# A depthwise tap moved from VectorE to a ScalarE product and an accumulating DMA, with a matrix streamed to make room

**Chip, cores, metric.** One core of one Trainium2 chip. The metric is the time of one execution in microseconds of device time, the median of several runs.

## The reference, cut to what matters

Input x is 32 images of 96 channels on 56 x 56 points. Three layers follow each other; the change touches the first, and one matrix of the second.

```python
# layer 0: expand 96 -> 576, depthwise 3x3, project 576 -> 96, residual
h = relu(bn(einsum('oc,bchw->bohw', w1, x)))
h = dwconv3x3(h, wdw)                  # nine taps per channel
h = relu(bn(h))
x = x + bn(einsum('oc,bchw->bohw', w2, h))
# layer 1a: layernorm, linear+relu, FFT over the 3136 tokens, a weighting with relu, inverse FFT, linear
# layer 1b: layernorm, a quantised two-layer MLP
```

## The kernel before

The 576 hidden channels are four groups of 128 on VectorE ("units") and a last group of 64 that TensorE does with diagonal matrices. A unit is one half image (28 rows, so 1568 points per channel) of one group: 8 units per image, 256 in all. Everything is written as generators that advance in common "ticks"; a unit takes four ticks, an image 32. Beside the units run the jobs of other images: `front` (projection, normalisation, transposes, start of the transform), `mid` (mixer), `back` (MLP).

```python
class Unit:
    def tap(self, n):                       # TAPS[0] is the centre (0, 0)
        dr, dc = TAPS[n]
        if n == 0:
            self.acc = ... w1.tile([128, R, S], F32, name="acc", bufs=7)
        ...                                 # rows ra:rb, columns ca:cb that the tap covers
        if n == 0:
            nc.scalar.activation(dst, src, AF.Identity, scale=w, bias=bd[...])
        else:
            nc.vector.scalar_tensor_tensor(dst, src, w, dst, ALU.mult, ALU.add)
    def finish(self):
        nc.scalar.activation(self.acc, self.acc, AF.Relu)

for u, after in zip(units, units[1:] + [None]):
    for q in range(4):                      # one tick each
        if q < 2 and after: after.expand(q)         # TensorE products, relu on ScalarE
        if q == 0 and last: last.finish()
        if q == 3 and after: after.tap(0)
        u.tap(2 * q + 1)
        u.tap(2 * q + 2)
        ...                                 # loads of the next image's halves, cut
        yield
    last = u

# front, cut: the projection reads the finished accumulators (and ends with an eviction on ScalarE),
# the norm is a chain of small VectorE and ScalarE steps, then TensorE transposes its result
#   pw <- w2T, acc | xt <- pw | bn_stats, va, sda, ra | xn <- xt, ra | ps <- ident, xn

jobs.append((T * i + 16 * (u // 2 + 1) + 1 + 4 * (u % 2), front(i, u)))
```

Two words used below: an *eviction* is the instruction (here mostly on ScalarE) that copies a TensorE result out of the tile TensorE wrote it to (`hs<-ps`, 128x812, took 936 ns in the kernel before); a DMA's *landing* is the time at which its data has arrived.

The text that is written gives an order to each engine only in part: the builder's scheduler moves instructions on an engine against each other where data allows. The traces are read here as each engine keeping the order of the list that comes out.

## Time and profile before

| | before |
|---|---|
| time | 5533.3 us, median of 3 runs (5532.4 to 5535.3) |
| TensorE busy | 4965 us, 90% |
| VectorE busy | 5018 us, 91% |
| ScalarE busy | 3801 us, 69% |
| mean granted TensorE clock | 0.955 of full speed |

The granted TensorE clock, in tenths, over 40 equal slices of the span:

```profile
PEclk9899999999999999999999999999999999999986
```

### The profile page before, as it was taken

To read this page: it belongs to the slowest core of one execution; us is meant where nothing else is said; L and a number is where in the kernel's file an instruction comes from. 1 tells how busy PE (TensorE), PEld (TensorE's weight loads), DVE (VectorE), ACT (ScalarE), POOL (GpSimd) and SP (SyncE) were. 2 spreads that over 40 slices of the span, in tenths; PEclk is the share of its full clock that TensorE was granted. 3 is DMA by queue.
4 is the path that set the end of the run, shared out by engine and by line. 5 is a ranking of instruction groups with operands and counts; after the bars stand their busy time and mean duration, and the time that the engine had idled before them with its cause. 6 is when DMAs were issued, how large, how long until landed. Compare 5 with 4: busy or idle time off the path is not lost.

```text
span 5533.0 us, 83297 instructions
## 1 busy us (share of the span) xinstructions
PE 4965.2 (90%) x32464; PEld 3804.1 (69%) x32464; DVE 5018.1 (91%) x8008; ACT 3800.6 (69%) x5574; POOL 75.6 (1%) x138
## 2 busy tenths in 40 slices
PE   5888999999999999999999999999999999999987
PEld 3566766766766766766766766766766767767765
DVE  7889999999999999999999999999999999999953
ACT  2456776776776776776777776776776777776765
POOL 0000000000000000000000000000000000000000
PEclk9899999999999999999999999999999999999986
DMA  2112332322232232232322332322332322332232
GB/s 51 48 50 64 86 87 74 86 85 77 81 88 79 82 87 79 82 87 78 87 84 76 85 88 74 88 83 77 86 87 76 88 81 77 88 84 78 78 106 66
DMA packets 320146, 440.94 MB, mean 80 GB/s; under 512 B 128244, under 2 KB 229176, under 8 KB 319640
## 3 DMA queue, kind: packets, MB, share of 16 engines
q1 hardware_dynamic: 319752, 435.62, 28.2%
q8 instruction: 255, 4.18, 0.3%
q14 instruction: 139, 1.14, 0.1%
HBM read 242.85 MB, written 192.68 MB: 79 GB/s over the span
## 4 chain that ended last, share of the span: by engine, by line
PE 77%; ACT 12%; DVE 7%; issue 2%; DMA 2%; SPq 0%; ACTq 0%
PE pd L459 13%; PE pw L511 13%; PE ps L351 12%; DVE acc L379 5%; PE ps L546 5%; PE ps L607 4%; PE ps L558 4%; PE ps L674 3%; PE ps L715 3%; ACT u L724 3%; PE ps L663 3%; PE pw L519 3%; PE ps L767 2%; PE ps L749 2%; PE ps L536 2%
## 5 line engine op out<-in xcount | busy, mean ns | idle before, releaser
L379 DVE SCALAR_TENSOR_TENSOR acc<-hs,wdw,acc 128x1540 f32<-128x1540 f32 (+3 forms) x2048 | 3674.1, 1799 | 55.3 <-ACT acc L377 48.2
L511 PE MATMUL pw<-w2T,acc 128*112 128x96 f32 x7168 | 912.9, 266 | 219.0 <-ACT acc L382 172.7
L511 PEld LDWEIGHTS pw<-w2T,acc 128*112 128x112 f32 x7168 | 824.2, 179 | 311.2 <-ACT acc L382 190.5
L351 PE MATMUL ps<-xs,w1T 96*128 96x406 f32 x2048 | 845.7, 533 | 21.5 <-ACT hs L358 17.5
L459 PE MATMUL pd<-hl,diag 128*128 128x385 f32 (+1 forms) x2304 | 825.4, 493 | 4.8 <-ACT al L468 1.8
L358 ACT ACTIVATE hs<-ps,b 128x812 f32<-128x812 f32 x512 | 479.2, 936 | 226.6 <-PE ps L351 176.7
L459 PEld LDWEIGHTS pd<-hl,diag 128*128 128x128 f32 x2304 | 420.6, 190 | 266.3 <-issue 39.3
L351 PEld LDWEIGHTS ps<-xs,w1T 96*128 96x128 f32 x2048 | 378.0, 201 | 196.7 <-issue 141.9
L377 ACT ACTIVATE acc<-hs,bd,wdw 128x1568 f32<-128x1568 f32 x256 | 434.9, 1699 | 4.3
L382 ACT ACTIVATE acc<-acc 128x1568 f32<-128x1568 f32 x256 | 385.3, 1505 | 42.7 <-DVE acc L379 42.6
L761 ACT ACTIVATE h<-h 128x784 fp8e5<-128x784 f16 x384 | 327.2, 855 | 79.0 <-DVE h L760 55.0
L724 ACT ACTIVATE u<-tt,mf,rf 112x96 fp8e5<-112x96 f32 x896 | 334.7, 454 | 55.8 <-DVE mf L494 55.6
L757 ACT ACTIVATE h<-ps 128x784 f16<-128x784 f32 x384 | 314.0, 820 | 60.2 <-PE ps L749 60.0
L546 PE MATMUL ps<-watt,xnT 97*112 97x192 f32 x1792 | 349.5, 334 | 1.8 <-ACT xnT L537 1.8
L558 PE MATMUL ps<-z,wa 112*112 112x384 f32 (+1 forms) x1024 | 344.0, 455 | 3.0 <-ACT z L550 2.9
L546 PEld LDWEIGHTS ps<-watt,xnT 97*112 97x112 f32 x1792 | 307.1, 183 | 50.2 <-issue 22.0
L607 PEld LDWEIGHTS ps<-wb,yb 112*128 112x128 f32 (+1 forms) x3584 | 308.5, 167 | 47.2 <-ACT h L757 18.4
L607 PE MATMUL ps<-wb,yb 112*128 112x112 f32 (+1 forms) x3584 | 329.5, 272 | 1.1 <-ACT y L771 0.8
L511 PE MATMUL pw<-w2T,al 128*112 128x96 f32 x1792 | 325.4, 264 | 0.0
L519 PE MATMUL pw<-idb,xs 97*112 97x96 f32 x1792 | 323.9, 263 | 0.0
L717 DVE TENSOR_TENSOR tt<-tt,ps 112x672 f32<-112x672 f32 x128 | 108.9, 851 | 214.1 <-PE ps L715 214.1
L537 ACT ACTIVATE xnT<-ps 96x784 f32<-96x784 f32 x128 | 104.6, 817 | 278.4 <-PE ps L536 278.2
(164 smaller groups left out, 7071.8 us busy)
## 6 DMA issues: line engine op xcount, KB each, us to landing
ydr<-ya SPq DMA_DIRECT2D x512, 147.0 KB
yb<-ydr SPq DMA_DIRECT2D x128, 588.0 KB
wd<-in_wd_dram SPq DMA_DIRECT2D x128, 349.1 KB
xs<-in_x_dram SPq DMA_DIRECT2D x64, 609.0 KB
tdr<-xt SPq DMA_DIRECT2D x128, 294.0 KB
tt<-tdr SPq DMA_DIRECT2D x128, 294.0 KB
gdr<-gc SPq DMA_DIRECT2D x256, 147.0 KB
gd<-gdr SPq DMA_DIRECT2D x128, 294.0 KB
```

What stands on the lines that cost most here:

```text
L351: nc.tensor.matmul(ps[:, j, 0:QW], lhsT=w1T[:, 128 * self.k : 128 * (self.k + 1)], rhs=xs[self.img, self.s][0:C, at : at + QW], start=True ...
L358: nc.scalar.activation(flat[:, 2 * h * QW : 2 * (h + 1) * QW].rearrange("p (j w) -> p j w", j=2), ps[:, :, 0:QW], AF.Relu, bias=b1[:, self ...
L377: nc.scalar.activation(dst, src, AF.Identity, scale=w, bias=bd[:, self.k : self.k + 1])
L379: nc.vector.scalar_tensor_tensor(dst, src, w, dst, ALU.mult, ALU.add)
L382: nc.scalar.activation(self.acc, self.acc, AF.Relu)
L459: nc.tensor.matmul(pv[:, :, ca:cb], lhsT=diag[:, n, :], rhs=hl[:, q : q + 7, ca + dc : cb + dc], start=(n == 0), stop=(n == 8),)
L511: nc.tensor.matmul(ps[:, q - a, 0:C], lhsT=src.rearrange("p r c -> p (r c)")[:, at : at + SK], rhs=w2T[:, k + (s if k == NK else 0), :], s ...
L519: nc.tensor.matmul(ps[:, q - a, 0:C], lhsT=xs[img, s][:, at : at + SK], rhs=idb, start=False, stop=True)
L546: nc.tensor.matmul(pv[0:SK, q - a, 0:HA], lhsT=xnT[:, q * SK : (q + 1) * SK], rhs=watt, start=True, stop=True)
L558: nc.tensor.matmul(ps[0:SK, j, 0 : (e - q) * HA], lhsT=wa, rhs=z[:, q:e, :], start=True, stop=True)
L607: nc.tensor.matmul(o, lhsT=lhsT, rhs=wb[:, g0 + G * s + q, :], start=True, stop=True)
L724: nc.scalar.activation(u8[:, q, :], t[:, q, :], AF.Identity, scale=r[:, q : q + 1], bias=m[:, q : q + 1], saturate=False,)
```

## The change

Intent: take one of eight taps off VectorE. The centre tap becomes a plain ScalarE product into a tile of its own, and an accumulating DMA adds that tile to the accumulator when the other taps are done. The vertical tap that covers all rows, until now VectorE's, becomes the ScalarE instruction that begins the accumulator. Since the accumulator is ready only when the DMA has landed, relu and front jobs move two ticks later, which needs an eighth accumulator; one of the input loads moves a tick later too. The room for the new tiles comes from streaming the transform matrix wb per mixer job and from single buffers for wd and gc.

```diff
+        def begin(self):
+            self.acc = ... w1.tile([128, R, S], F32, name="acc", bufs=8)
+            dr = 1 - 2 * self.s
+            nc.scalar.activation(self.acc, self.hs[:, o : o + R, :], AF.Identity, scale=self.weight(dr, 0), bias=...)
+        def centre(self):
+            self.p = w1.tile([128, R, S], F32, name="centre")
+            nc.scalar.activation(self.p, self.hs[:, o : o + R, :], AF.Copy, scale=self.weight(0, 0))
+        def taps(self, q):
+            ...                              # two of the seven remaining taps per tick
+            if q == 3:
+                nc.gpsimd.dma_start(out=self.acc..., in_=self.p..., accum_op=ALU.add)
...
+                if q == 1:
+                    u.centre()
-                if q == 0 and last:
+                if q == 2 and last:
                     last.finish()
...
+        yield
+        yield
         last.finish()
...
-    wb = cst([SK, NP, SK], "wb")            # whole matrix, loaded once
+        wb = w1.tile([SK, 2 * G, SK], F32, name="wb")    # in mid: one half, loaded per job
-            gc = w2.tile(...)
+            gc = w1.tile(...)
-        wd = w2.tile(...)
+        wd = w1.tile(...)
-            jobs.append((T * i + 16 * (u // 2 + 1) + 1 + 4 * (u % 2), front(i, u)))
+            jobs.append((T * i + 16 * (u // 2 + 1) + 3 + 4 * (u % 2), front(i, u)))
```

More of the change, by code (lines that the diff above doesn't have):

```diff
@@ L192, in tile_kernel @@
     ws = load([SK, SK], "ws", d["ws"])
-    wb = cst([SK, NP, SK], "wb")
-    nc.sync.dma_start(out=wb.rearrange("p k m -> p (k m)"), in_=d["wb"])
     b1 = cst([128, NK + 1], "b1")
@@ L363, in expand, with weight @@
             )
-        def tap(self, n):
-            dr, dc = TAPS[n]
-            o = R * self.s - base[self.s]
-            if n == 0:
-                self.acc = acc[self.img, self.s, self.k] = w1.tile([128, R, S], F32, name="acc", bufs=7)
-            at = 3 * (dr + 1) + dc + 1
-            w = wdw[:, self.k, at : at + 1]
-            ra, rb = max(0, -(o + dr)), min(R, XR - o - dr)
-            ca, cb = max(0, -dc), S - max(0, dc)
-            src = self.hs[:, ra + o + dr : rb + o + dr, ca + dc : cb + dc]
-            dst = self.acc[:, ra:rb, ca:cb]
-            if n == 0:
-                nc.scalar.activation(dst, src, AF.Identity, scale=w, bias=bd[:, self.k : self.k + 1])
-            else:
-                nc.vector.scalar_tensor_tensor(dst, src, w, dst, ALU.mult, ALU.add)
+        def weight(self, dr, dc):
+            at = 3 * (dr + 1) + dc + 1
+            return wdw[:, self.k, at : at + 1]
@@ new lines, in begin @@
+        def begin(self):
+            self.acc = acc[self.img, self.s, self.k] = w1.tile([128, R, S], F32, name="acc", bufs=8)
+            dr = 1 - 2 * self.s
+            o = R * self.s - base[self.s] + dr
+            nc.scalar.activation(
+                self.acc,
+                self.hs[:, o : o + R, :],
+                AF.Identity,
+                scale=self.weight(dr, 0),
+                bias=bd[:, self.k : self.k + 1],
+            )
+        def centre(self):
+            self.p = w1.tile([128, R, S], F32, name="centre")
+            o = R * self.s - base[self.s]
+            nc.scalar.activation(self.p, self.hs[:, o : o + R, :], AF.Copy, scale=self.weight(0, 0))
@@ new lines, in taps @@
+        def taps(self, q):
+            rest = [t for t in TAPS[1:] if t != (1 - 2 * self.s, 0)]
+            o = R * self.s - base[self.s]
+            for dr, dc in rest[2 * q : 2 * q + 2]:
+                ra, rb = max(0, -(o + dr)), min(R, XR - o - dr)
+                ca, cb = max(0, -dc), S - max(0, dc)
+                src = self.hs[:, ra + o + dr : rb + o + dr, ca + dc : cb + dc]
+                dst = self.acc[:, ra:rb, ca:cb]
+                nc.vector.scalar_tensor_tensor(dst, src, self.weight(dr, dc), dst, ALU.mult, ALU.add)
+            if q == 3:
+                nc.gpsimd.dma_start(
+                    out=self.acc.rearrange("p r c -> p (r c)"),
+                    in_=self.p.rearrange("p r c -> p (r c)"),
+                    accum_op=ALU.add,
+                )
@@ L389, in conv_ticks @@
         units[0].expand(1)
-        units[0].tap(0)
+        units[0].begin()
         last = None
@@ L395, in conv_ticks @@
                     after.expand(q)
-                if q == 0 and last:
+                if q == 1:
+                    u.centre()
+                if q == 2 and last:
                     last.finish()
                 if q == 3 and after:
-                    after.tap(0)
-                u.tap(2 * q + 1)
-                u.tap(2 * q + 2)
+                    after.begin()
+                u.taps(q)
                 if q == 2 and u.s == 0 and u.k == NK - 1 and u.img + 1 < nimg:
                     load_half(u.img + 1, 0)
-                if q == 2 and u.s == 1 and u.k == NK - 2 and u.img + 1 < nimg:
+                if q == 3 and u.s == 1 and u.k == NK - 2 and u.img + 1 < nimg:
                     load_half(u.img + 1, 1)
@@ L586, in mid @@
         g0 = 2 * G * half
+        wb = w1.tile([SK, 2 * G, SK], F32, name="wb")
+        nc.sync.dma_start(
+            out=wb.rearrange("p k m -> p (k m)"), in_=d["wb"][:, g0 * SK : (g0 + 2 * G) * SK]
+        )
         yb = []
@@ L606, in spread @@
                         o, lhsT = pv[:, q, 0:SK], yb[s][:, q, 0:128]
-                    nc.tensor.matmul(o, lhsT=lhsT, rhs=wb[:, g0 + G * s + q, :], start=True, stop=True)
+                    nc.tensor.matmul(o, lhsT=lhsT, rhs=wb[:, G * s + q, :], start=True, stop=True)
             return pv[:, 0:G, 0:SK]
@@ L693, in mid @@
             nc.tensor.matmul(ps[0:SK, 1, 0:n], lhsT=wc, rhs=p[:, n:], start=True, stop=True)
-            gc = w2.tile([SK, G * C], F32, name="gc")
+            gc = w1.tile([SK, G * C], F32, name="gc")
             nc.scalar.activation(gc.rearrange("p (j w) -> p j w", j=2), ps[0:SK, :, 0:n], AF.Copy)
@@ L704, in back @@
     def back(img, u):
-        wd = w2.tile([KD, G * SK], F32, name="wd")
+        wd = w1.tile([KD, G * SK], F32, name="wd")
         nc.sync.dma_start(out=wd, in_=d["wd"][:, G * SK * u : G * SK * (u + 1)])
```

## The prediction

The forecast came to 166.7 us per image, 5340 us in all. Its sum has 14 us of stalls per image, reckoned with L, the DMA's time from issue to landing, at 7.5 us (between 6 and 9).

> **What bounds the kernel now.** I read the page's first part (busy shares), then a table of stretches, one image long each, then the groups by shape, then the waits, and last the chain of work inside a stretch of 60 us. The program runs 32 images of equal work as one software pipeline; start-up and drain aside an image takes about 173 us (5533 / 32).[...]
>
> ```profile
> PE 4965.2 (90%) x32464; PEld 3804.1 (69%) x32464; DVE 5018.1 (91%) x8008; ACT 3800.6 (69%) x5574; POOL 75.6 (1%) x138
> ...
> q1 hardware_dynamic: 319752, 435.62, 28.2%
> ```
>
> ```profile
> core 0: us, PE busy (x) PEld busy (x) DVE busy (x) ACT busy (x) POOL busy (x), PEclk, DMA share, GB/s
> ...
> 2173.00:2346.00 173.00, 159.88 (x1074) 123.47 (x1073) 163.79 (x268) 122.72 (x180) 2.19 (x4) 0.98 0.30 85
> 2346.00:2519.00 173.00, 159.88 (x1062) 123.13 (x1060) 162.64 (x263) 122.81 (x180) 2.20 (x4) 0.97 0.29 82
> ```
>
> Two engines are full: of 173 us VectorE is busy about 162.5 and TensorE 160. ScalarE has 50 us of room, GpSimd does nothing, the DMA engines are 29% busy. The groups by shape say what VectorE does:
>
> ```profile
> L379 DVE SCALAR_TENSOR_TENSOR acc<-hs,wdw,acc 128x1540 f32<-128x1540 f32 x1024 | 1852.2, 1812 | 20.3 <-ACT acc L377 16.9
> ...
> L379 DVE SCALAR_TENSOR_TENSOR acc<-hs,wdw,acc 128x1568 f32<-128x1568 f32 x256 | 472.5, 1846 | 1.2
> ...
> L377 ACT ACTIVATE acc<-hs,bd,wdw 128x1568 f32<-128x1568 f32 x256 | 434.9, 1699 | 4.3
> ...
> L382 ACT ACTIVATE acc<-acc 128x1568 f32<-128x1568 f32 x256 | 385.3, 1505 | 42.7 <-DVE acc L379 42.6
> ```
>
> Eight of nine taps of each of the 256 depthwise units (8 per image) are VectorE work. The waits show that TensorE's gaps come mostly from lateness there: the projection waits for a finished accumulator, a transpose for a normalised tile.
>
> ```profile
> PEld pw L511 <- ACT acc L382: 190.5, 41, 9.0
> ...
> PE pw L511 <- ACT acc L382: 172.7, 37, 8.8
> ...
> PE ps L536 <- DVE xn L531: 104.4, 35, 6.4
> ```
>
> But TensorE's busy time is not all throughput. In the chain of one stretch its pieces touch, and give the real pace:
>
> ```profile
> 2010.61 1.95 PE pd L459 x6
> 2012.56 0.97 PE pw L511 x10
> ...
> 2015.58 1.38 PE ps L351 x4
> 2016.96 1.36 PE ps L674 x14
> ```
>
> Six L459 products take 1.95 us, 0.325 us each, where the group's mean for one is 493 ns (the modelled ends overlap). Summing the groups at such paces (L459 72 x 0.325, L351 64 x 0.345, the projection 336 x 0.098, the other products about 68 us) I get some 147 us per image that TensorE needs. So VectorE is the bound by need, 162.5, and TensorE follows with 147 to 160.
>
> [...]
>
> **The change part by part.** (1) VectorE loses the full-size tap: 8 x 1.846 = 14.8 us per image, so need 162.5 - 14.8 = 147.7. The vertical tap that covers all rows becomes the first ScalarE product, at the same 1568 elements, so no change there. (2) ScalarE gains a Copy with a scale over 1568 elements, between the relu's 1.505 and the begin's 1.699: 8 x 1.6 = 12.8 us, so 123 + 13 = 136 us. That is beside other work by sum, but in its queue. (3) A DMA of 128 x 1568 x 4 = 803 KB per unit. Queue 1 moved 435.62 MB in 28.2% of the 16 engines' 5533 us: 279 GB/s while busy. A copy of 803 KB at that rate is 2.9 us[...]. (4) The product buffer is single, so the next unit's centre product waits for this DMA to land; the relu stands right behind it in ScalarE's order. That wait is the real cost. In the built order of the changed kernel I followed it for the eight units of an image: from a unit's last tap, add up the VectorE work that stands ahead of the first VectorE instruction that needs ScalarE work after the next centre, and take off the ScalarE work between, at the durations above. That leaves room for L of 5.0, 6.1, 2.8, 5.5, 11.9, 6.7, 7.1 and 5.5 us. What L exceeds stalls VectorE: at 6 us 5 us per image, at 7.5 us 14, at 9 us 24. (5) The wb matrix streamed: 64 x 702 KB = 45 MB more, asked for three ticks (16 us) before use, on a queue with room: nothing. wd with one buffer: nothing, since the gd tile loaded beside it is single already and is released by the same products. gc with one buffer: ScalarE may wait for the first store of a pair, one tick (5.4 us) earlier; up to 1 us, twice per image. The front jobs' two ticks later keep the distance to the later relu; eight accumulators pay for it.
>
> **Sum.** Before: 162.5 of need plus 10.5 of VectorE's idle = 173. After: 147.7 of need, 14 of stalls on the DMA, and of the 10.5 idle perhaps 5, because ScalarE's and TensorE's lateness hides behind the same stalls (this is a choice, not a measurement). 166.7 us per image, 6.3 less; over about 31 images in steady state 195 us: **5340 us**, 3.5% faster.
>
> **The rivals.** (A) The DMA is quick, 6 us or less: stalls fall to 5 us, need is 147.7 beside TensorE's 147, and TensorE becomes the bound near 160: about 5130 to 5200. For it: [...]DMA engines idle two thirds of the time. (B) The DMA takes 9 us or more: 147.7 + 24 + 4 = 176 us, so 5600 to 5650, and at 10 us (31 of stalls) over 5800; the wait at the centre product takes the place of the tap removed. For it: [...]the present traffic comes on bursts of 73% share. Against it: the single buffer would hardly have been kept had the wait been that long. (C) TensorE is the bound already, as the page's chain (77% TensorE) suggests, and what VectorE gives up only widens its idle: then within 2%. Against: the 172.7 us wait of the projection and the touching pieces at 147 us of pace. (D) ScalarE, 136 us plus waits in order, delays the evictions that TensorE waits for; this is in the 14 + 5 and could double it.
>
> **Range and chances.** L from 6 to 9 us spans 160 to 176 us per image, that is 5170 to 5650; widened a little at the top for (D): 5170 to 5680. L below about 8 us gives over 2% (break-even with the present 173 is near 8.7): chance 0.58. Within 2%: 0.22, (C) or L near 8.5. Slower: 0.20, for (B) and (D).
>
> **What would show it.** Right: tap instructions 2048 to 1792, VectorE busy near 4550 us; ScalarE near 4220 with 256 more products of 1.6 us; a software queue with 206 MB[...]; the main new wait is the centre product on the DMA, in total 1 to 2.5 us per unit (300 to 600 us), least in the fifth unit of an image; TensorE's wait for the relu gone or smaller; no wait that counts on wb, wd or gc. Wrong: no wait at the centre and TensorE above 95% busy (A); waits of over 4 us per unit there (B); VectorE idle spread over waits for TensorE with its pieces touching (C); the relu or an eviction named as what TensorE waits for, in more than the 173 us of now (D); a much longer tap[...].

## The result, and the profile after

5882.5 us, median of 4 runs (5878.2 to 5893.9): **6.3% slower**, ratio 1.0633, 95% interval 1.0615 to 1.0652. The result is correct. (Ratios in this document are the mean time of one kernel's fast runs over the mean of the other's fast runs of the same rounds, so not quite the ratio of the medians quoted.)

From the page of the kernel after: busy shares, granted clock, and the new queue.

```profile
PE 5264.2 (89%) x32464; PEld 3983.0 (68%) x32464; DVE 4626.6 (79%) x7752; ACT 4152.4 (71%) x5830; POOL 332.4 (6%) x394
...
PEclk8899988998889998889998899988899988899986
...
q0 software_dynamic: 36864, 205.54, 17.6%
```

VectorE did lose its work: 5018 to 4627 us. TensorE has exactly as many instructions as before, and yet is busy 299 us longer. The clock line says how: 8 stands where 9 stood. It was 0.5 for 1155 us in place of 500. If work at half clock goes at half the pace, as the two pieces below have it, half of the extra 655 us is lost work, 327 us (an estimate), which is about what the busy time gained. The rest of the 350 us is idle: span less busy is 619 us after, 568 before.

What a halved clock does, from the timeline of the kernel after (start, duration, engine, line, what, count): two equal pieces of expansion work, 4 us apart, the first nearly all at half clock (the trace has it from 2042.58 to 2049.41), the second at full. Of the first, 2.11 us ran at half clock and 0.47 at full; 2.11 / 2 + 0.47 is 1.53, the length of the second.

```profile
2047.30 2.58 PE L348 MATMUL ps<-xs,w1T 96*128 96x406 f32 x4
...
2051.35 1.53 PE L348 MATMUL ps<-xs,w1T 96*128 96x406 f32 x4
```

When the clock halves, the trace of the kernel after shows: all 112 spells of half clock begin on one fixed grid of 3.41 us, and 37 of them last 10.24 us, 32 last 13.65 and 29 last 6.83, so three, four and two times 3.41. A wholly idle window was not needed: one less than half busy was enough. Take the windows of that grid between 100 and 5150 us that ran at full clock, and TensorE's busy share in each (from modelled ends, so roughly):

| busy share of the window, kernel after | windows | clock halved right after |
|---|---|---|
| under 50% | 65 | 65 |
| 50 to 60% | 27 | 23 |
| 60 to 70% | 16 | 2 |
| 70% and more | 1101 | 0 |

Under 50% it halved every time in the kernel before (34 of 34) and in runs 7, 8, 9, 15, 17 and 18 too (11, 36, 85, 22, 38 and 33). Nor did it take one long gap: 45 of the 112 spells, 351 of the 1155 us, have no gap of 2 us or more in the two windows before them. A gap of 3.4 us did it in all 57 cases counted further down.

The waits show who makes the gaps. First ScalarE's wait on the new DMA, then TensorE's list (engine, tile and line waiting, releaser: total us, times, longest us):

```profile
ACT centre L382 <- DMA acc<-centre: 323.4, 104, 7.5
```

```profile
PE ps L775 <- ACT uT L764: 157.0, 68, 5.4
PE pw L533 <- ACT acc L401: 132.6, 36, 5.1
PE pw L533 <- ACT xt L547: 84.9, 94, 6.3
```

The wait that the prediction named, TensorE for the relu, went only from 173 to 133 us, and two others, for evictions of ScalarE, grew beside it: from 59 to 157 us (uT) and from 43 to 85 us (xt). How one leads to another is in the timeline of the kernel after (square brackets: idle before it and what ended that):

```profile
2079.19 0.86 POOL L394 DMA_DIRECT2D acc<-centre  x1 [19.50 <-ACT V L656]
...
2089.30 1.60 ACT L382 ACTIVATE centre<-hs,wdw 128x1568 f32<-128x1568 f32 x1 [3.80 <-DMA acc<-centre]
...
2091.66 0.81 PE L775 MATMUL ps<-uT,w1q 96*128 96x392 fp8e5 x2 [4.24 <-ACT uT L764]
```

and in the stretches around it (us; busy per engine; then granted clock, DMA share, GB/s):

```profile
2084.00:2090.00 6.00, 3.42 (x36) 3.27 (x35) 5.38 (x5) 2.20 (x6) 0.00 (x0) 1.00 0.67 158
2090.00:2096.00 6.00, 4.34 (x13) 1.75 (x13) 2.63 (x4) 5.07 (x7) 1.07 (x1) 0.53 0.00 0
2096.00:2102.00 6.00, 6.00 (x23) 3.41 (x22) 4.38 (x6) 4.23 (x7) 0.58 (x1) 0.50 0.37 100
```

The DMA is issued at 2079.19, and the next unit's centre product, whose tile the DMA still reads, waits until 2089.30 (a long landing; the median is 5.9 us). For 3.80 us ScalarE evicts nothing. Behind the product stands an eviction (uT, at 2090.81) that the MLP's first product needs. Its own input was complete at 2086.60, and yet it didn't pass the waiting product: ScalarE kept its order. TensorE is empty for 4.24 us, from 2087.42 on. At 2090.4 its clock halves, and stays so for 13.65 us. So this ScalarE wait of 3.80 us cost TensorE a gap of 4.24 us and then up to half of the 12 us from 2091.66 to 2104.02 (an estimate from the pace above).

### The profile page after: what moved, and what is told of

It is laid out like the page before. It is cut to its first block, busy times and chain, and to the rows that moved or that the text cites. A ratio compares the mean times of both kernels' runs of the same rounds, so it can differ in the third digit from the quotient of the medians.

```text
span 5883.5 us, 84263 instructions
## 1 busy us (share of the span) xinstructions
PE 5264.2 (89%) x32464; PEld 3983.0 (68%) x32464; DVE 4626.6 (79%) x7752; ACT 4152.4 (71%) x5830; POOL 332.4 (6%) x394
## 3 DMA queue, kind: packets, MB, share of 16 engines
q0 software_dynamic: 36864, 205.54, 17.6%
## 5 line engine op out<-in xcount | busy, mean ns | idle before, releaser
L392 DVE SCALAR_TENSOR_TENSOR acc<-hs,wdw,acc 128x1540 f32<-128x1540 f32 (+2 forms) x1792 | 3213.1, 1794 | 217.3 <-ACT acc L371 208.6
L348 PE MATMUL ps<-xs,w1T 96*128 96x406 f32 x2048 | 833.4, 531 | 38.0 <-ACT hs L355 33.1
L481 PE MATMUL pd<-hl,diag 128*128 128x385 f32 (+1 forms) x2304 | 851.3, 502 | 3.0 <-ACT al L490 1.4
L382 ACT ACTIVATE centre<-hs,wdw 128x1568 f32<-128x1568 f32 x256 | 410.9, 1605 | 323.5 <-DMA acc<-centre 323.4
L348 PEld LDWEIGHTS ps<-xs,w1T 96*128 96x128 f32 x2048 | 394.2, 204 | 276.7 <-issue 188.4
L394 POOL DMA_DIRECT2D acc<-centre x256 | 220.5, 861 | 4320.4 <-DVE acc L392 888.2
L568 PE MATMUL ps<-watt,xnT 97*112 97x192 f32 x1792 | 434.2, 390 | 30.6 <-ACT xnT L559 30.6
L568 PEld LDWEIGHTS ps<-watt,xnT 97*112 97x112 f32 x1792 | 357.7, 214 | 86.2 <-ACT xnT L559 44.0
L633 PEld LDWEIGHTS ps<-wb,yb 112*128 112x128 f32 (+1 forms) x3584 | 347.4, 181 | 54.3 <-issue 44.8
L775 PE MATMUL ps<-uT,w1q 96*128 96x392 fp8e5 x768 | 234.1, 398 | 157.0 <-ACT uT L764 157.0
L633 PE MATMUL ps<-wb,yb 112*128 112x112 f32 (+1 forms) x3584 | 370.9, 288 | 1.3 <-ACT y L797 0.8
L654 DVE SCALAR_TENSOR_TENSOR sb<-ps,cw,V 128x784 f32<-128x784 f32 x192 | 197.6, 1029 | 204.2 <-ACT V L642 187.3
```

The lines of the kernel that those rows point to most:

```text
L348: nc.tensor.matmul(ps[:, j, 0:QW], lhsT=w1T[:, 128 * self.k : 128 * (self.k + 1)], rhs=xs[self.img, self.s][0:C, at : at + QW], start=True ...
L382: nc.scalar.activation(self.p, self.hs[:, o : o + R, :], AF.Copy, scale=self.weight(0, 0))
L392: nc.vector.scalar_tensor_tensor(dst, src, self.weight(dr, dc), dst, ALU.mult, ALU.add)
L481: nc.tensor.matmul(pv[:, :, ca:cb], lhsT=diag[:, n, :], rhs=hl[:, q : q + 7, ca + dc : cb + dc], start=(n == 0), stop=(n == 8),)
L568: nc.tensor.matmul(pv[0:SK, q - a, 0:HA], lhsT=xnT[:, q * SK : (q + 1) * SK], rhs=watt, start=True, stop=True)
L633: nc.tensor.matmul(o, lhsT=lhsT, rhs=wb[:, G * s + q, :], start=True, stop=True)
```

## The experiments

Three theories at first. **T1**: the wait of the centre product on the DMA starves TensorE. **T2**: the two ticks by which relu and front jobs moved do it, with no DMA needed. **T3**: the extra transfers and the single buffers of the streaming do it. Later ones (T4 to T7) are in the expectations. Some kernels give a wrong result (a tap or a DMA is left out); they are marked.

**1. Streaming alone.** Before, with wb per job and wd, gc in one buffer.

> The kernel before with the second part of the change alone: wb streamed per mixer job, wd and gc with one buffer; all nine taps as before. Theory T1 (ScalarE's wait for the accumulating DMA starves TensorE, whose clock then halves) and theory T2 (the later relu and front jobs are to blame) both expect the time of before, 5533 within 1%. Theory T3 (the extra transfers and the single buffers slow other work) expects a good part of the 350 us: over 5650.

Measured 5528.9 us, ratio 0.9993 (0.9978 to 1.0007). Streaming costs nothing, so T3 falls; the kernel is the base for others.

**2. The later ticks alone.** All eight taps stay on VectorE.

```diff
-                if q == 0 and last:
+                if q == 2 and last:
-    ... + 1 + 4 * (u % 2), front(i, u)))
+    ... + 3 + 4 * (u % 2), front(i, u)))      # and bufs=8 for acc
```

> The same, and in addition the change's new timing: relu two quarters of a unit later, front jobs two ticks later, eight accumulators; still eight taps on VectorE, no accumulating DMA. T1 expects about the time of before, 5480 to 5600, with the granted clock at 0.94 or more. T2 expects most of the loss: over 5700 and a clock near 0.91. T3 as in the run with the streaming alone.

Measured 5778.0 us, ratio 1.0441 (1.0423 to 1.0458). No DMA, no product, and two thirds of the loss is there. In TensorE's waits the transposes that need the normalised tile went up from 104.4 us:

```profile
PE ps L536 <- DVE xn L531: 280.1, 65, 11.3
```

**3 and 4. Fixed order on ScalarE.** The centre product and the relu may not be moved by the scheduler; in the second the product also stands a tick later.

```diff
-            nc.scalar.activation(self.p, ...)
+            tc.keep_in_program_order(nc.scalar.activation(self.p, ...))     # and the relu
```

> The changed kernel with the centre product and the relu kept in program order on ScalarE, so that the builder can't move them up: same work, same DMA. By the same count over the built order that gave 2.8 to 11.9 us of room before VectorE suffers, the room is now 8.5 to 12.9 us, all above the 5.9 us that the DMA takes. T1 expects the wait for the DMA at the centre to fall from 323 us to under 60, the clock to return to 0.95 and the time to 5150 to 5450. T2 expects no gain, 5800 to 5950, since relu and front jobs stand as late as before. T3 expects no gain either, since the traffic is the same.

> As the run before this one, with the centre product one quarter later, just ahead of the relu: room 8.5 to 24 us. T1 expects the same as that run within 1.5% (the wait is gone in both, so more room buys nothing), perhaps slower, since the relu stands later in ScalarE's order. T2 and T3 expect 5800 to 5950.

Measured 5967.3 us, ratio 1.0785 (1.0769 to 1.0801), and 5945.6 us, ratio 1.0744 (1.0716 to 1.0771). In the first the wait on the DMA is all but gone (323 to 16 us of the centre product), and the time is longer still, because TensorE now waits for the normalised tile as in run 2 (40 us in the kernel after):

```profile
PE ps L560 <- DVE xn L555: 206.3, 36, 10.0
```

T1 expected 5150 to 5450, so T1 alone doesn't explain the loss. These two runs change the whole order, so they price nothing.

**5 and 6. Filler products against the halved clock.** Five unused products of 512 columns ahead of one projection per image, and in the changed kernel also ahead of one MLP product.

```diff
+            for _ in range(5 if u == 2 and a == 0 else 0):
+                tc.keep_in_program_order(nc.tensor.matmul(ps..., lhsT=ident[:, 0:SK], rhs=diag...[:, 0:512], ...))
```

> The kernel before, with five unused products of 512 columns (each overwritten by the group's own first product) kept in program order just ahead of the third front job's first group, where TensorE idled 4.7 us in every image and its clock then halved.[...] Theory T4: in all six kernels so far the span is about 5290 us plus half of the time at half clock (502 to 1339 us), so TensorE bounds all of them and the clock makes the difference. T4 expects the throttled time to fall from 502 to under 250 us and the time to 5290 to 5450. Rival T5, the halved clock is only a symptom of the waits and costs nothing by itself: 5533 to 5680, no gain or a loss of the fillers' time. The pinned order can blur this by 1%.

> The changed kernel with such fillers at its two gaps per image of 3.8 us (third front job's first group) and 4.2 us (first back job, ahead of the hidden layer). T4 expects throttled time well under 1157 us and the time lower by half of what it loses: 5400 to 5750. T5 expects 5880 to 6100.

Measured 5889.4 us, ratio 1.0643, and 6265.4 us, ratio 1.1324. Both far worse: with the products pinned, the transposes' wait for the normalised tile rose from 104 to 291 us in the first, and its span less busy to some 710 us. There the half clock rose to 826 us; in the second it fell from 1155 to 1086 us while the time rose by 383. As a test of the clock (T4 against T5) they failed; that the gap halves the clock is seen in the traces, not shown by an intervention.

**7. The relief alone (wrong result).** The kernel before without the full vertical tap.

```diff
-            else:
+            elif (dr, dc) != (1 - 2 * self.s, 0):
                 nc.vector.scalar_tensor_tensor(...)
```

> The kernel before with one of VectorE's eight taps left out (the full-size vertical one) and nothing in its place; timing and jobs as before, wrong result on purpose. This is what relief of VectorE alone is worth. The prediction's view, VectorE is the bound by need and 14.8 us per image come off: at or under 5200. T4, TensorE is the bound: 5290 plus half the throttled time, so 5290 to 5560, however the gaps fall, with VectorE idle for what it gained.

Measured 5180.0 us, ratio 0.9360 (0.9346 to 0.9374), mean clock 0.977.

```profile
PE 4877.6 (94%) x32464; PEld 3713.0 (72%) x32464; DVE 4596.4 (89%) x7752; ACT 3774.7 (73%) x5574; POOL 73.5 (1%) x138
```

VectorE bounded the kernel before: taking 461 us of tap time from it gives 353 us of time, and TensorE's busy time falls too, since it waits less and its clock is halved for 241 us only. T4 (TensorE bounds every kernel, at 5290 us plus half of the half clock) expected 5290 to 5560 here and falls.

**8. The change without its DMA (wrong).** Everything else as in the kernel after.

> The changed kernel without the accumulating DMA: the centre product is still computed on ScalarE and its tile is not added (wrong result on purpose). No wait for a DMA, no extra SBUF traffic; relu and front jobs as late as in the change. T1 (the wait for the DMA): under 5600. T2 (the later relu and front jobs): 5700 to 5900, near the 5778 of the shifted kernel. T4: whatever it is, within 1% of 5290 plus half its throttled time.

Measured 5737.3 us, ratio 1.0371 (1.0354 to 1.0388). The DMA costs 145 us here. The product on ScalarE and the later ticks, with seven taps on VectorE, cost 557 us over run 7.

**9. The change at the early ticks.** Relu at q == 1, front jobs at their old ticks; correct.

```diff
-                if q == 2 and last:
+                if q == 1 and last:
-    ... + 3 + 4 * (u % 2), front(i, u)))
+    ... + 1 + 4 * (u % 2), front(i, u)))
```

> The changed kernel with the front jobs at their old ticks and the relu one quarter later than in the kernel before (instead of two quarters and two ticks): centre product, DMA, streaming all kept, correct result. So far 7 taps at the old timing gave 5180, 8 taps at the new timing 5778, 7 taps and the product without the DMA at the new timing 5737. Theory T2, the later front jobs are what costs: 5200 to 5500, faster than before, the clock over 0.95. T1, the wait for the DMA costs most (the room by the built order is 1.6 to 11 us here, against 5.9 for the DMA, no better than in the change): 5750 or more. If neither, the product on ScalarE is the cost and the time lies between.

Measured 5697.5 us, ratio 1.0303 (1.0277 to 1.0329): 185 us less than the change. ScalarE's wait on the DMA is longer than in the kernel after, and TensorE's longest waits are these:

```profile
ACT centre L382 <- DMA acc<-centre: 549.1, 160, 9.5
```

```profile
PE ps L632 <- ACT hs L355: 110.4, 28, 4.3
PE ps L348 <- ACT y L796: 86.5, 28, 4.4
PE ps L802 <- ACT pj L708: 84.5, 28, 3.6
```

Each comes 28 times, so about once per image, and each names an eviction. One of them in the timeline: the product waits 3.39 us, two ScalarE instructions later, of which the second is the eviction, TensorE resumes after 3.95 us.

```profile
2182.87 1.60 ACT L382 ACTIVATE centre<-hs,wdw 128x1568 f32<-128x1568 f32 x1 [3.39 <-DMA acc<-centre]
2184.38 0.19 ACT L509 ACTIVATE sdf<-vf 112x7 f32<-112x7 f32 x1
2184.47 0.92 ACT L355 ACTIVATE hs<-ps,b 128x812 f32<-128x812 f32 x1
...
2185.44 0.83 PE L632 MATMUL ps<-wb,yb 112*64 112x112 f32 x6 [3.95 <-ACT hs L355]
```

**10. All jobs two ticks later.** As the change, with `last_channels`, `mid` and `back` moved as well, so that the jobs keep their distances to each other; correct.

> The changed kernel with all the other jobs (last channels, mid, back) two ticks later as well, so that they stand to the front jobs as before, and only to the depthwise units two ticks later. T2a, the front jobs now collide with the other jobs: 5250 to 5550. T2b, what costs is the distance from the depthwise units, not the jobs among each other: 5800 or more.

Measured 5987.2 us, ratio 1.0822 (1.0806 to 1.0838). The loss doesn't come from the front jobs having moved against the other jobs alone.

**11 and 12. Timing and product apart, with seven taps (both wrong).** Run 2 without the vertical tap; and run 1 without it and with the centre product on ScalarE, unused.

> The new timing with seven taps and nothing in place of the eighth (wrong result on purpose): neither product nor DMA. Beside the 5180 of seven taps at the old timing and the 5778 of eight at the new. T2: 5400 to 5700, so the timing costs 250 us or more with seven taps too and eats the whole relief. If it is under 5300, the timing costs little once VectorE is relieved, and the product on ScalarE is what makes the 5737 of the run without DMA.

> Seven taps at the old timing, with the streaming, and the centre product computed on ScalarE but used by nobody (wrong result on purpose): 256 more ScalarE operations of 1.6 us, no DMA. T2 expects 5180 to 5350: ScalarE has room for 12.8 us per image. The rival, that the product's place in ScalarE's order costs as much as the tap on VectorE: 5450 or more.

Measured 5449.9 us, ratio 0.9849 (0.9835 to 0.9864), and 5338.4 us, ratio 0.9647 (0.9633 to 0.9662). Against the 5180 us of run 7 the later ticks cost 270 us and the product 158 us. Together they cost 557 (run 8), 129 more than the sum. Run 12 has 33 TensorE gaps of 3.4 us or more, counted in its trace as in the table further down, where run 7 has 6: that the product costs more here than at the early ticks of run 15 (158 against 70 us, with 5 gaps) fits that.

**13 and 14. The DMA at the start of the unit.** Begin, centre product and DMA of the next unit together at q == 2 (13) or q == 1 (14), relu and front jobs at their old ticks; correct.

```diff
-                if q == 3 and after:
+                if q == 2 and after:
                     after.begin()
+                    after.centre()
+                    after.add()
```

> The change with the DMA at the start of a unit instead of its end: begin and centre product of the next unit on ScalarE in the third quarter, the DMA at once, all seven taps after it; relu and front jobs at their old places; correct result. Only VectorE's first tap waits for the DMA, some 5 to 10 us after its issue, and ScalarE waits for it only four quarters later. Theory T6, what costs is the wait in ScalarE's order (and the later relu that makes room for it), not the DMA: 5300 to 5450, near the 5338 of the unused product, faster than before. Rival T7, the DMA's traffic costs by itself: 5480 or more.

> The same one quarter earlier (begin, product and DMA in the second quarter), so that the DMA has landed even longer when VectorE comes: T6 expects no difference from the third quarter beyond 1.5%, unless VectorE's first tap still waits there; T7 the same loss in both.

Measured 5836.9 us, ratio 1.0564 (1.0516 to 1.0611), and 5864.8 us, ratio 1.0599 (1.0583 to 1.0615). T6 expected 5300 to 5450 for run 13 and missed. The wait changed its engine: now VectorE's first tap waits for the DMA's landing (here run 13; 490.9 us in run 14).

```profile
DVE acc L392 <- DMA acc<-centre: 490.3, 178, 20.2
```

**15. Early ticks without the DMA (wrong).**

> The run with the old front ticks and the relu one quarter later (5697), without the DMA; wrong result on purpose. T6: 5320 to 5450, so that the DMA and its wait are worth 250 us or more at that place. If it stays above 5550, the relu's place one quarter later was what cost, and the DMA little.

Measured 5250.1 us, ratio 0.9491 (0.9475 to 0.9507). Against it run 9 says that the DMA costs 447 us at the early ticks; run 8 says that the later ticks cost 487 us without the DMA. TensorE's wait for the normalised tile in the two, run 15 and then run 8:

```profile
PE ps L551 <- DVE xn L546: 15.5, 5, 4.7
```

```profile
PE ps L552 <- DVE xn L547: 187.4, 34, 7.2
```

34 waits against 5, so once per image at the later ticks. One of them in the timeline of run 8, and the clock around it:

```profile
2156.06 1.77 DVE L392 SCALAR_TENSOR_TENSOR acc<-hs,wdw,acc 128x1485 f32<-128x1485 f32 x1
2157.74 0.16 DVE L149 TENSOR_TENSOR tmpa<-ra 112x7 f32<-112x7 f32 x1
2157.93 0.17 DVE L150 SCALAR_TENSOR_TENSOR tmpa<-tmpa,va 112x7 f32<-112x7 f32 x1
2158.14 0.17 DVE L151 SCALAR_TENSOR_TENSOR ra<-tmpa,ra 112x7 f32<-112x7 f32 x1
2158.49 1.76 DVE L392 SCALAR_TENSOR_TENSOR acc<-hs,wdw,acc 128x1485 f32<-128x1485 f32 x1 [0.19 <-ACT acc L371]
2160.17 0.85 DVE L547 TENSOR_TENSOR xn<-xt,ra 112x672 f32<-112x672 f32 x1
...
2161.17 1.51 PE L552 MATMUL ps<-ident,xn 112*96 112x112 f32 x7 [6.19 <-DVE xn L547]
```

```profile
2155.00:2161.00 6.00, 0.00 (x0) 0.00 (x0) 5.75 (x9) 6.00 (x7) 0.00 (x0) 0.70 0.39 102
2161.00:2167.00 6.00, 5.83 (x25) 5.74 (x26) 5.89 (x5) 1.63 (x3) 0.00 (x0) 0.50 0.00 0
```

The small steps of the norm stand between taps of 1.77 us in VectorE's order, and the transposes are the next thing in TensorE's. For 6 us TensorE has nothing at all. At the early ticks the same transposes wait for VectorE only five times in all. This wait is not the whole price: of run 8's 108 spells of half clock 70, with 723 of 1138 us, have no gap of 2 us or more in the two windows before them. The clock halved there after all 36 windows that were under half busy, so short idle times were enough; what makes them I haven't followed up.

**16. The traffic alone, first attempt (wrong).** Seven taps at the old ticks, and per unit an accumulating DMA of the same size between two spare tiles, started by a GpSimd copy of one accumulator column.

> Seven taps at the old timing, no product, and per unit one accumulating DMA of the same size between two spare tiles after the unit's last tap, for which nobody but GpSimd waits (wrong result on purpose). T6: 5160 to 5260, near the 5180 of bare seven taps. T7: 5320 or more.

Measured 5331.3 us, ratio 0.9635 (0.9621 to 0.9649), 151 us over run 7. But VectorE's taps waited 176 us in a way that run 7 doesn't show (31 times, up to 5.8 us); that the copy's hold on the accumulator does it is my guess, not shown. So 151 us, though in the range of T7 (5320 or more), is no clean price of the traffic.

**17. The traffic alone, second attempt (wrong).** Run 15 with the DMA, from the centre product's tile, but into a spare tile that nobody reads; seven accumulators.

```diff
-                    out=self.acc.rearrange("p r c -> p (r c)"),
+                    out=ddst.rearrange("p r c -> p (r c)"),
```

> The early timing with the same accumulating DMA of the same size from the same source, but into a spare tile that no instruction reads, and with seven accumulators: all the traffic and all of GpSimd's issuing, and no wait except the next unit's centre product some 20 us later. The result is wrong on purpose. If the traffic itself costs (T7): 5400 us or more, against 5250 without the DMA and 5697 with the real one, with longer taps or longer evictions. If only the wait for the landing costs (T1): within 1.5% of 5250, with no wait of the centre product on the DMA above 50 us in all.

Measured 5358.8 us, ratio 0.9687 (0.9671 to 0.9704): 109 us over run 15, between the two expectations (under 1.5%, or over 150 us). The wait on the DMA is 56.8 us. The long taps take 1816 ns, as without the DMA (1815), so VectorE isn't slowed. TensorE is busy 78 us longer and its clock is halved for 145 us more, although its gaps of 3.4 us did not grow (5 and 4): 78 of this run's 81 spells have no such gap at them. What makes the shorter idle times I have not settled. One thing more differs from the real DMA: nothing holds this one back to the last tap. The trace shows 251 of its 256 issues released by the centre product, so it runs earlier in the unit.

**18. Two tiles for the centre product.** Run 9 with its real DMA, a second buffer for the product and seven accumulators in place of eight (the room of one pays for the other); correct.

```diff
-            self.acc = ... name="acc", bufs=8)
+            self.acc = ... name="acc", bufs=7)
-            self.p = w1.tile([128, R, S], F32, name="centre")
+            self.p = w1.tile([128, R, S], F32, name="centre", bufs=2)
```

> The early timing with the real DMA, two buffers for the centre product and seven accumulators: the centre product no longer waits for the DMA of the unit before it, so the only wait left is the relu's, for the accumulator itself, and it stands right behind the centre product in ScalarE's order. Correct. If the reuse of the single product buffer is what costs: the wait falls from 549 us by the length of the centre product for each wait (160 waits x 1.6 us = some 250 us), and the time falls to some 5450, which is faster than the kernel before. If the landing ahead of the relu is what costs, wherever the wait is put down: the relu waits for it in its turn with 300 to 550 us in all, and the time stays between 5600 and 5700.

Measured **5431.1 us, ratio 0.9819** (0.9804 to 0.9834): 266 us less than run 9, and 1.8% faster than the kernel before, which is less than the 2% that the prediction calls faster, but outside what chance explains. ScalarE now waits at the relu, for the sum it needs in any case, with the centre product done meanwhile. Of TensorE's three waits on the list of run 9, those of L632 and L348 are gone (nothing over 10 us is left of either), and L802 has half:

```profile
ACT acc L401 <- DMA acc<-centre: 373.8, 131, 8.3
```

```profile
PE pw L532 <- ACT acc L401: 118.6, 64, 7.4
PE ps L802 <- ACT pj L708: 46.4, 29, 2.2
```

**The steps in a row.** Each row adds one thing to the row above, with these exceptions. The step to run 15 adds the product on ScalarE together with the streaming (nothing, by run 1), the relu and one input load a tick later and an eighth accumulator. The step to run 18 also puts the DMA behind the last tap. The last step moves two things, as named. Accumulators are seven in the first two rows and in runs 17 and 18, eight in the others. Gaps are TensorE's of 3.4 us or more, counted in the trace between 100 and 5150 us; the last column is the time at half clock in the whole trace.

| kernel | us | step | TensorE busy | gaps | half clock, us |
|---|---|---|---|---|---|
| before | 5533 | | 4965 | 35 | 500 |
| seven taps (run 7) | 5180 | -353 | 4878 | 6 | 241 |
| product on ScalarE, early (15) | 5250 | +70 | 4904 | 5 | 306 |
| DMA that nobody needs (17) | 5359 | +109 | 4981 | 4 | 451 |
| DMA into the accumulator, two product tiles (18) | 5431 | +72 | 4959 | 8 | 441 |
| one product tile (9) | 5698 | +266 | 5080 | 40 | 731 |
| relu a tick, front jobs two ticks later (after) | 5882 | +185 | 5264 | 57 | 1155 |

The two steps that lose the change are the last two, and in both the gaps and the half clock rise together; in the step to run 17 the half clock rises without them. The last is nearly all TensorE's pace: busy time rises 184 us, idle time 17.

The steps depend on their order. With the later ticks first, those cost 487 us and the DMA with its one tile 145; so the two overlap (487 and 447 us, each without the other, 632 together). That TensorE's gap of one hides that of the other would explain it, but was not shown.

## Why the prediction was wrong

**VectorE is the bound by need, and removing a tap relieves it.** Right. Predicted 14.8 us per image, 459 us over 31 images; tap time fell by 461 us (3674 to 3213), and the time by 353 when nothing else was changed (run 7). The rest of the relief met TensorE.

**The DMA's duration, 6 to 9 us, at 7.5, and the wait it makes.** In the kernel predicted the median landing was 5.9 us, just under the range; in runs 9 and 18, with other orders, 7.4 and 7.5. Its share of the DMA engines was 17.6%, where 25% was reckoned. The wait was forecast well: 300 to 600 us of the centre product on the DMA, 323 measured. Predicted stalls of 14 us per image at 7.5 us make 434 us; the DMA cost 447 at the early ticks. Predicted 5 at 6 us, so 155; it cost 145 at the later ones. That both agree is partly luck: the rule counted the order of the changed kernel, not that of run 9, and it priced VectorE's waits, while 109 of the 447 us are there without any wait for the sum, and 266 arise from TensorE's gaps behind the single product tile. So the wait was right, and where it was priced was not: on VectorE alone, and not on the evictions behind it in ScalarE's order. Rival A, for a fast landing, fell: at 5.9 us it gave 5130 to 5200.

**"The front jobs' two ticks later keep the distance to the later relu; eight accumulators pay for it."** This is the first step that failed. It was priced at nothing and measured at +185 us in the row above, +487 without the DMA, +270 with seven taps and no product, +244 with all eight taps. Distance to the relu was the only distance I looked at. What I looked past is what else each engine has in its order when the front job's norm runs; run 8 shows it for one wait, and the rest of the price is not followed up.

**"Of the 10.5 idle perhaps 5", marked as a choice.** It credited 5.5 us per image, 170 us, to lateness hiding behind stalls. No step of the row shows this credit, and VectorE's idle time in the kernel after is 5883 - 4627 = 1256 us, 39 per image, where the sum had 19. But that the DMA costs 145 us behind the later ticks and 447 without them shows that some lateness does hide, so this step is not shown to be wrong by itself.

**ScalarE's product, "beside other work by sum, but in its queue".** The queue was named and priced at nothing. It is not free: 70 us at the early ticks, 158 in run 12, as time in ScalarE's order before evictions (this reason is argued, not tested).

**Streaming costs nothing.** Right, run 1.

Put together over 31 images: predicted -459 for the tap, +434 for stalls, -170 for idle, so -195. Measured -353, +447 (109 + 72 + 266), +70 for the product and +185 for the ticks: +349. Of the 544 us between them 106 are the relief, 13 the DMA, 170 the credited idle, 70 the product and 185 the ticks.

**The rivals.** (D) came closest: ScalarE's order delays evictions that TensorE waits for. It "could double" 19 us per image. What it lacked was the second half: a gap of TensorE has a price after it has ended, the half clock. The kernel before showed that already (its gap of 4.68 us ended at 2118.99, and the clock was 0.5 from 2117.74 to 2127.98). The prediction noted TensorE's 147 us of pace and 160 of busy time and put the difference down to overlapping modelled ends alone, without asking how the clock entered. Its own sign was met: TensorE's three waits for evictions listed above come to 374 us (275 before), where it had set 173 for the one of the relu. (B) had the right wait and the wrong duration for it: at 7.4 us, not 9, run 9 was at its 5600 to 5650 and over. (C) fell with run 7.

**Slips in its sums.** By its own 31 images, 160 us per image is 5130 us, not 5170, and 176 is 5626, not 5650; break-even, 20.3 us of stalls, comes by its own list of rooms at 8.4 us, not 8.7. None of them decides anything here.

**What stays open.** That the halved clock, and not the gaps alone, carries the cost is read from the traces: equal products take 2.58 and 1.53 us, and TensorE's busy time rises with the time at half clock. The fillers that should have tested it made another wait longer (104 to 291 us in run 5). How the bare traffic costs 109 us is open. So is whether the relu's tick or the front jobs' ticks matter more, since they were always moved together from run 9 to the change. A hint: between runs 12 and 15 the relu moves a tick later and the front jobs don't, and run 15 is 88 us faster (the vertical tap, an accumulator and a load change too). And every edit lets the builder order all engines anew, so each price is that of a whole order.

## What to carry to other kernels

Before work is moved to an idle engine, look at what stands behind it in that engine's order: here a wait for a DMA there (3.80 us in the kernel after, 3.39 us in run 9) held the eviction behind it, and TensorE paid with a gap (4.24 and 3.95 us) and then with half clock: in the kernel after it came after all 65 windows of 3.41 us that were less than half busy, and 98 of the 112 spells lasted 6.83 to 13.65 us. So give a tile that a DMA reads a second buffer before anything else (266 us here), and put the wait at the instruction that needs the result. A change of timing "to make room" is a change of its own: measure it alone, and sum TensorE's time at half clock before and after; its gaps of 3.4 us or more alone miss much of it (3 of the 81 spells of run 17 have one).

## What the runs measured of the hardware

- Half clock: gaps of TensorE came from ScalarE held at a DMA for another engine's tile (3.39 us there, 3.95 us on TensorE, run 9) and from a norm chain between long taps on VectorE (6.19 us, run 8). In the kernel after, equal products took 2.58 us, most of it at half clock, against 1.53 us; 98 of 112 spells of half clock lasted two, three or four times 3.41 us; the clock halved after all 65 windows that were under half busy, and 45 of 112 spells had no gap of 2 us or more in the two windows before.
- The accumulating DMA, 803 KB on 128 partitions of 6272 B: from issue to landing 5.9 us in the median in the kernel after (5.7 to 11.2), 6.3 in run 16 (5.8 to 10.8), 7.4 and 7.5 in runs 9 and 18. Issuing it took GpSimd 859 ns in the median, 1067 at most, in the kernel after. VectorE's long taps (128x1540) took 1816 ns with the DMA (runs 9 and 17) and 1815 without (run 15).
- The centre products on ScalarE, 411 us in all, cost 70 us (run 15) to 158 us (run 12) of the kernel's time, with ScalarE busy only 69% before.
- With one buffer for the DMA's source tile the landing became a wait of the engine that fills it next: 549 us at the centre product in run 9, and 266 us of the kernel's time against two buffers (run 18).
